# A fused attention and sign-weight FFN layer: partition folds of the dot products, sums of o in rows, signs kept in DRAM, relu values split in another place

## The chip, the cores and the metric

The kernel runs on one core of one Trainium2 chip, as one launch. The metric is the device time in microseconds (us) of that core. Engines are named as in the profile: PE is TensorE's matmul row and PEld its weight loads, DVE is VectorE, ACT is ScalarE, POOL is GpSimd, SP is SyncE. SP and POOL issue the DMAs, and only POOL issues those that add to their destination.

## The reference

x has 2048 tokens of 512 values. All arithmetic is float32.

```python
xn = layernorm(x)
# attention: 16 heads of 128, four lags
q, k, v = (causal_conv4(silu(xn @ W)) for W in (Wq, Wk, Wv))   # depthwise, 4 taps
z, a, b = xn @ Wz, xn @ Wa, xn @ Wb
q, k = rotate(q), rotate(k)                                    # rotary embedding
q, k = q / max(norm(q), 1e-12), k / max(norm(k), 1e-12)        # per head
out = 0
for s in range(4):                                             # k, v, a of s tokens earlier
    attn = sum_d(q * lag(k, s)) / sqrt(128)
    out += attn * sigmoid(lag(a, s) * b) * lag(v, s)
out = out * rsqrt(mean(out * out) + 1e-6) * norm_w * silu(z)   # mean over all 2048 columns
s = out @ Wout
# FFN with weights reduced to their signs
h = relu((xn @ sign(up).T) * up_scale)
g = silu((h @ sign(down).T) * down_scale * output_scale)
return x + s * g
```

## The kernel before, in words

**Layout.** Channels lie on partitions and tokens in columns. The 2048 tokens are four blocks of 512 (TB), the 16 heads eight pairs (NP). A pair's 256 channels are two halves j of 128 partitions; partitions 0 to 63 of both halves are the first head, 64 to 127 the second. xnT holds the normalised tokens, transposed.

**Order of work.** Tile decides the order on ACT, POOL and SP; `InOrder` (L68) keeps PE and DVE in the order in which the program is written, and gives all their instructions line 76, so that groups are told apart by tile names. The stages are:

- *Front stage.* `step(p, -1)` (L524) for p = 0 to 7 makes queries and keys of block 0: `queries` (L297) projects q, convolves it; `products` (L320) does the same for k, turns q for the lags (L305), squares q and k, and multiplies q by the lagged k. Beside it the FFN of block 0 is computed in four groups of G = 4 chunks: in even steps `ups` (L617), the first two chunks between q and k (`beside_q`), the last two after the step; in odd steps `downs` (L623), likewise in halves. `fetch` (L605) loads raw weights, ACT makes their signs (L612). `in_two_terms` (L576) splits a relu value into hid_hi and hid_lo on DVE (a cast and a subtraction), both of which PE multiplies.
- *Main loop.* `step(p, b)` for b = 0 to 2 makes q and k of block b+1 and the rest of block b: `values` (L434), z (L441), `weighted` (L450: the four lags of v times coefficients broadcast from DRAM, tiles bc, te, o), oz = o times norm_w times silu(z) (L481), and every second step the output projection of two pairs (L495), whose results (part, three buffers) POOL adds up in s_dram (L513, L515).
- *Last attention block.* L667 to L734: values, z and outputs of block 3. Beside it the up weights are loaded once more and reduced to signs (up_raw, L686 to L693), two chunks per step, and two chunks of the next FFN block are computed ahead (L728).
- *FFN of blocks 1 to 3.* L737 on: down weights are loaded and reduced to signs (L741), then for each chunk f up (ph), relu, split, down (pf). `ends` (L744) does the final gating.

**Dot products.** `products` multiplies q by four lags of k into pr (128 partitions, 4 lags x 512 tokens), once for each half j (L342 to L347). In blocks 1 to 3 POOL's DMA adds the second to the first (L349); in block 0, made in the front stage, DVE does (L352). `sum_dots` (L371) then sums over partitions on PE, pair by pair and a step later: four matmuls with a 32-column indicator `of_head`, one for each lag, in the four column tiles, all pairs accumulating in one bank. `coefficients` (L423) multiplies the dots by the norms and the gate and writes them to DRAM.

**Sums of o.** The squares of o are added over pairs by POOL's DMA (L478). `sums_of_o` (L379) sums them over partitions at the end of a block: eight matmuls with the squares as weights and one column of ones, giving tokens on partitions in so, copied to ss_acc. After the last block ACT and DVE turn ss_acc into rms (L733, L734), in DVE's order ahead of the FFN's splits.

**Queues.** POOL issues its DMAs in order, an instruction that waits holds those behind it; so does SP. In the main loop POOL's are sq<-sq, pr<-pr, ss<-o, s_dram<-part, and at some steps ab_dram and xnT.

Of the kernel before, what the change touches and what calls it, by code (L numbers as in the profile page):

```python
# [44 lines left out]
P = 128  # L45
# [36 lines left out]
def recurrent_layer(ctx: ExitStack, tc: tile.TileContext, a: dict, out: bass.AP):  # L82
# [11 lines left out]
    ones = const.tile([P, 1], F32, name="ones")  # L94
# [12 lines left out]
    ab_dram = dram.tile([LW, HALO + S], F32, name="ab_dram")  # L107
    f_dram = dram.tile([TB, HID], F32, name="f_dram")
# [19 lines left out]
    def small_loads():  # L128
        nc.sync.dma_start(conv_w, a["conv_w"])
        nc.sync.dma_start(w_ab, a["w_ab"])  # L130
        nc.sync.dma_start(ab_dram[:, 0:HALO], no_ab)
        nc.sync.dma_start(turns, a["turns"])
        nc.sync.dma_start(of_head, a["of_head"])
        nc.sync.dma_start(norm_w, a["norm_w"])
        nc.sync.dma_start(up_scale, a["up_scale"])
# [37 lines left out]
    def statistics(b, c):  # L173

        if c == 0:
            means[b] = qks.tile([P, TC, 2], F32, tag="mv", name=f"mv{b}", bufs=2)
            nc.sync.dma_start(xnT[:, :, HALO + b * TB : HALO + (b + 1) * TB], a["xT"][b])
        t = b * TC + c
        x_in = qks.tile([P, HID], F32, tag="x_in", name=f"x_in{t}", bufs=2)
        nc.sync.dma_start(x_in, a["x"][t * P : (t + 1) * P, :])  # L180
        st = qks.tile([P, 6], F32, tag="st", name=f"st{t}", bufs=2)
        dve.bn_stats(st, x_in)
        dve.bn_aggr(means[b][:, c, :], st)
# [43 lines left out]
    def gate(b):  # L227

        g = qks.tile([P, TB], F32, tag="gate", name=f"gate{b}", bufs=2)
        other = qks.tile([P, TB], F32, tag="rk", name=f"gate_b{b}", bufs=1)  # L230
        for r in range(0, P, H):
            lo = HALO + b * TB - r // LW
            nc.sync.dma_start(g[r : r + H, :], ab_dram[0:H, lo : lo + TB])
            nc.sync.dma_start(other[r : r + H, :], ab_dram[H:, HALO + b * TB : HALO + (b + 1) * TB])
        dve.tensor_tensor(g, g, other, ALU.mult)
        nc.scalar.activation(g, g, AF.Sigmoid)
        gates[b] = g
# [82 lines left out]
    def products(p, b, q, between=None):  # L320

        n = f"_{p}_{b}"
        load(qks, "k", p, b)
        q0 = q[:, LAGS - 1]
        k = with_halo(qks, "k", "k", 1, p, b)
        raw = raw_of(qks, "k", p, b)
        if p % 2 == 0:
            sum_squares()
        convolve(1, p, raw, k[:, :, HALO:])
        keep_halo("k", k, p, b)  # L330
        if between:
            between()
        turn(q)

        sq = [qks.tile([P, 2, TB], F32, tag=f"sq{j}", name=f"sq{j}" + n, bufs=2 - j) for j in range(2)]
        for j in range(2):
            nc.scalar.activation(sq[j][:, 0], q0[:, j], AF.Square)
            nc.scalar.activation(sq[j][:, 1], k[:, j, HALO:], AF.Square)
        nc.gpsimd.dma_start(sq[0], sq[1], accum_op=ALU.add)
        squares_due.append((p, sq[0]))  # L340
        prs = []
        for j in range(2):  # L342
            pr = qks.tile([P, LAGS, TB], F32, tag="pr", name=f"pr{j}" + n, bufs=2)
            k0 = k[:, j, 0:TB]
            k_lags = bass.AP(k0.tensor, k0.offset, [k0.ap[0], [1, LAGS], k0.ap[1]])
            dve.tensor_tensor(pr, q[:, :, j, :], k_lags, ALU.mult)
            prs.append(pr)  # L347
        if b:
            nc.gpsimd.dma_start(prs[0], prs[1], accum_op=ALU.add)  # L349
        else:  # L350

            dve.tensor_tensor(prs[0], prs[0], prs[1], ALU.add)  # L352
        dots_due.append((p, prs[0]))

    def add(to, s, p, src, start, stop):

        rows = to[LW * s : LW * s + LW, :]
        pe.matmul(rows, of_head[:, p, :], src, start=start, stop=stop, tile_position=(0, LW * s))

    def sum_squares():  # L360

        if not squares_due:
            return
        if squares_due[0][0] == 0:
            banks["squares"] = sums.tile([P, TB], F32, tag="squares", name="squares")
        for p, sq in squares_due:
            for i in (1, 0):
                add(banks["squares"], 2 * (p % 2) + 1 - i, p, sq[:, i, :], p < 2, p >= NP - 2)
        squares_due.clear()

    def sum_dots():  # L371

        p, pr = dots_due.pop(0)
        if p == 0:
            banks["dots"] = sums.tile([P, TB], F32, tag="dots", name="dots")
        for s in range(LAGS):
            add(banks["dots"], s, p, pr[:, LAGS - 1 - s, :], p == 0, p == NP - 1)

    def sums_of_o(b):  # L379

        so = mm.tile([P, TC], F32, tag="mm", name=f"so{b}")
        for c in range(TC):
            for j in range(2):
                pe.matmul(
                    so[:, c : c + 1],
                    squares[b][:, j, c * P : (c + 1) * P],
                    ones,
                    start=(j == 0),
                    stop=(j == 1),
                )  # L390
        nc.scalar.copy(ss_acc[:, b * TC : (b + 1) * TC], so)  # L391
# [4 lines left out]
    def norms(b):  # L396

        sqs = banks["squares"]
        r = qks.tile([P, HALO + TB], F32, tag="r", name=f"r{b}", bufs=1)[0 : 2 * LW]
        nc.scalar.copy(r[0:LW, 0:HALO], kept_r)  # L400
        sq2 = qks.tile([2 * LW, TB], F32, tag="sq2", name=f"sq2{b}", bufs=1)
        nc.scalar.copy(sq2, sqs[2 * LW :, :])
        norm = r[:, HALO:]
        dve.tensor_tensor(norm, sq2, sqs[0 : 2 * LW, :], ALU.add)
        dve.tensor_scalar_max(norm, norm, NORM_MIN * NORM_MIN)
        nc.scalar.activation(norm, norm, AF.Sqrt)
        rows[b] = r
# [33 lines left out]
    def gates_of_output(p, b):  # L441

        load(vs, "z", p, b)
        wo = vs.tile([P, 2, HID], F32, tag="wo", name=f"wo_{p}_{b}", bufs=3)
        nc.sync.dma_start(wo, a["wo"][p])
        z = vs.tile([P, 2, TB], F32, tag="z", name=f"z_{p}_{b}", bufs=1)
# [77 lines left out]
    def step(p, b, beside_q=None):  # L524
# [9 lines left out]
        due = len(dots_due)  # L534
        products(p, b + 1, q, (lambda: norms_in_rows(b)) if change and b else None)
        if change:
# [4 lines left out]
            due = 0  # L541
# [5 lines left out]
        if due:  # L547
            sum_dots()
# [53 lines left out]
    with tc.tile_pool(name="pre", bufs=1, side="right") as pre:  # L602
        signs = {}

        def fetch(g, which):  # L605

            for f in range(G * g, G * g + G):
# [4 lines left out]
                nc.scalar.activation(sign, raw, AF.Sign)  # L612
                signs[which, f] = sign
# [30 lines left out]
        for p in range(NP):  # L644
            g = p // 2
            if p == 0:
                step(p, -1)
                fetch(0, "up")
                ups(0, G)
            elif p % 2 == 0:  # L650
                step(p, -1, lambda: ups(G * g, G * g + 2))
                ups(G * g + 2, G * g + G)
            else:
                step(p, -1, lambda: downs(g, 0, 2))
                downs(g, 2, TC)
# [24 lines left out]
    up = ffw.tile([P, NFC, KC, P], F32R, name="up")  # L680
    first_down = ffw.tile([P, 2, HID], F32R, name="first_down")
# [4 lines left out]
    def fetch(to, name, src, shape):  # L686

        raw = ffw.tile(shape, F32, tag="raw", name=name, bufs=4)
        nc.sync.dma_start(raw, src)
        return lambda: nc.scalar.activation(to, raw, AF.Sign)  # L690

    def fetch_up(f):
        return fetch(up[:, f], f"up_raw{f}", a["up"][f], [P, KC, P])  # L693

    def fetch_down(to, f):
        return fetch(to, f"down_raw{f}", a["down"][f], [P, HID])

    def ups_ahead(f, ph):
        hids.append((1, f, up_projection(ph, ffw, f, 1, up[:, f], xs)))


    fetched = []
    for p in range(NP + 1):
        if 0 < p < NP:
            load(vs, "v", p, last)
            raw = raw_of(vs, "v", p, last, 1)
        if p:
            z, wo = gates_of_output(p - 1, last)
        if p % 2 == 1:
            output_projections()  # L710
        if p < NP:
# [5 lines left out]
        for sign in fetched:  # L717
            sign()
        if p < NP:
            fetched = [fetch_up(2 * p), fetch_up(2 * p + 1)]  # L720
        else:
            fetched = [fetch_down(first_down[:, f], f) for f in range(2)]
        if p == 4:
            xs = in_two_terms(ffw, tokens(1), "xs", 1, [P, KC, TB], "xs1")
    for sign in fetched:
        sign()
# [10 lines left out]
    with tc.tile_pool(name="ff", bufs=1, side="right") as ff, tc.tile_pool(  # L737
        name="ph", bufs=3, space=PSUM
    ) as phs, tc.tile_pool(name="pf", bufs=1, space=PSUM) as pfs:
        down = ff.tile([P, NFC - 2, HID], F32R, name="down")  # L740
        for f in range(2, NFC):  # L741
            fetch_down(down[:, f - 2], f)()
# [32 lines left out]
        def down_projection(c, f, terms):  # L775
            for i, term in enumerate(terms):
# [3 lines left out]
                    first_down[:, f] if f < 2 else down[:, f - 2],  # L780
# [5 lines left out]
        for b in range(1, NTB):  # L786
            pf = [pfs.tile([P, HID], F32, name=f"pf{c}") for c in range(TC)]
            for f in range(2, NFC + 2):
# [3 lines left out]
                if ub < NTB:  # L792
                    ph = phs.tile([P, TB], F32, name="ph")
                    hids.append((ub, uf, up_projection(ph, ffw, uf, ub, up[:, uf], xs)))
                if b == 1 and f == 2:
                    scale, gate = ends(0)
                if b == 1 and f in (4, 6, 8, 10):
                    scale(f // 2 - 2)
                    gate(f // 2 - 2)
# [12 lines left out]
            if b == last:  # L812

                for cs in (0, 1), (2, 3):
# [41 lines left out]
def _constants():  # L856
# [9 lines left out]
    of_head = (row[None, None, :] == 2 * np.arange(NP)[None, :, None] + half[:, None, None])  # L866
    return {
        "turns": turns.astype(f),
# [23 lines left out]
```

## Time and profile before

| what | value |
|---|---|
| median of 3 runs | 1468.28 us (1465.31 to 1468.89) |
| the profiled execution, device time | 1469.35 us |
| its span in the profile | 1467.6 us |
| granted TensorE clock, mean | 0.99 |
| front stage, first ph to first pv | 27.8 to 237.4 us |
| main loop, to the last block's first pv | 237.4 to 1084.5 us |
| last attention block, to its last po | 1084.5 to 1280.1 us |
| FFN of blocks 1 to 3, to the last pf | 1282.2 to 1459 us |
| two software and hardware DMA queues | 81.80 MB and 161.84 MB |

How to read it: times in the trace are counted from the span's start. A row of a group reads line, engine, operation, out<-in, shapes and count, then busy us, mean ns of one, and the idle time just before. One float32 matmul of 512 columns gives two records, one of the sign-weight FFN (fp32r) one. "A <- B" among the waits means that A's engine stood still until B was done. The DMA share is the mean busy share of the 16 DMA engines.

### The profile page before, as it was taken

To read this page: it belongs to the slowest core of one execution; us is meant where nothing else is said; L and a number is where in the kernel's file an instruction comes from. 1 tells how busy PE (TensorE), PEld (TensorE's weight loads), DVE (VectorE), ACT (ScalarE), POOL (GpSimd) and SP (SyncE) were. 2 spreads that over 40 slices of the span, in tenths; PEclk is the share of its full clock that TensorE was granted. 3 is DMA by queue.
4 is the path that set the end of the run, shared out by engine and by line. 5 is a ranking of instruction groups with operands and counts; after the bars stand their busy time and mean duration, and the time that the engine had idled before them with its cause. 6 is when DMAs were issued, how large, how long until landed. Compare 5 with 4: busy or idle time off the path is not lost. (4 is left out here: it accounts for less than half of the span.)

```text
span 1467.6 us, 12650 instructions
## 1 busy us (share of the span) xinstructions
PE 1428.4 (97%) x4080; PEld 699.4 (48%) x4080; DVE 1184.2 (81%) x1327; ACT 631.5 (43%) x1213; POOL 160.0 (11%) x205
## 2 busy tenths in 40 slices
PE   7999889999999999999999999999998999999997
PEld 4545444434444444444444444444434444578886
DVE  6888889999999878999898689998886968245454
ACT  6456445444444444444444444434343433242122
POOL 0101101010201110102011101010100011100000
PEclk9999999999999999999999999999999999999999
DMA  8747538877888677768886787687748976562120
GB/s 277 203 101 152 121 74 214 198 203 189 189 218 176 153 172 192 194 169 188 212 185 147 159 208 192 169 181 184 162 101 200 256 239 151 84 224 68 40 87 29
DMA packets 95857, 244.44 MB, mean 167 GB/s; under 512 B 15344, under 2 KB 15728, under 8 KB 92720
## 3 DMA queue, kind: packets, MB, share of 16 engines
q1 hardware_dynamic: 71024, 161.84, 36.1%
q0 software_dynamic: 24768, 81.80, 30.7%
q8 instruction: 32, 0.52, 0.1%
q14 instruction: 33, 0.27, 0.1%
HBM read 157.60 MB, written 27.28 MB: 126 GB/s over the span
## 5 line engine op out<-in xcount | busy, mean ns | idle before, releaser
L76 PE MATMUL pz<-xnT,wz 128*128 128x512 f32 x512 | 228.2, 598 | 4.5 <-ACT up L690 4.5
L76 PE MATMUL po<-wo,oz 128*128 128x512 f32 x512 | 225.6, 598 | 3.2 <-DVE oz L76 3.2
L76 PE MATMUL pq<-xnT,wq 128*128 128x512 f32 x512 | 228.0, 598 | 0.7 <-ACT xnT L169 0.7
L76 PE MATMUL pv<-xnT,wv 128*128 128x512 f32 x512 | 226.7, 595 | 0.9 <-ACT up L690 0.9
L76 PE MATMUL pk<-xnT,wk 128*128 128x512 f32 x512 | 225.3, 592 | 0.0
L76 DVE SCALAR_TENSOR_TENSOR q<-rq,conv_w,q 128x512 f32<-128x512 f32 x192 | 141.9, 749 | 49.9 <-ACT q L280 45.3
L76 DVE SCALAR_TENSOR_TENSOR k<-rk,conv_w,k 128x512 f32<-128x512 f32 x192 | 143.0, 751 | 45.8 <-ACT k L280 41.2
L76 PEld LDWEIGHTS po<-wo,oz 128*128 128x128 f32 x512 | 96.9, 191 | 130.6 <-issue 112.8
L76 PEld LDWEIGHTS pz<-xnT,wz 128*128 128x128 f32 x512 | 96.1, 190 | 132.3 <-issue 117.3
L76 DVE SCALAR_TENSOR_TENSOR v<-rv,conv_w,v 128x512 f32<-128x512 f32 x192 | 141.4, 750 | 20.8 <-ACT v L280 16.2
L76 PEld LDWEIGHTS pv<-xnT,wv 128*128 128x128 f32 x512 | 95.4, 189 | 129.7 <-issue 114.8
L76 PEld LDWEIGHTS pq<-xnT,wq 128*128 128x128 f32 x512 | 97.7, 191 | 122.9 <-issue 119.4
L76 PEld LDWEIGHTS pk<-xnT,wk 128*128 128x128 f32 x512 | 96.7, 189 | 121.1 <-issue 116.6
L76 DVE TENSOR_TENSOR pr<-q,k 128x2048 f32<-128x2048 f32 x64 | 143.8, 2288 | 1.1
L76 DVE SCALAR_TENSOR_TENSOR q<-q,turns 128x1024 f32<-128x1024 f32 (+1 forms) x128 | 127.1, 1014 | 2.3
L76 DVE TENSOR_TENSOR o<-o,te 128x1024 f32<-128x1024 f32 x96 | 117.6, 1225 | 3.3
L76 DVE TENSOR_TENSOR te<-v,bc 128x1024 f32<-128x1024 f32 x96 | 117.0, 1219 | 0.0
L597 ACT ACTIVATE hid<-ph,up_scale 128x512 f32<-128x512 f32 x64 | 43.9, 685 | 116.2 <-PE ph L76 115.7
L76 DVE CAST hid_hi<-hid 128x512 fp32r<-128x512 f32 x64 | 27.1, 424 | 76.3 <-ACT hid L597 76.3
L268 ACT ACTIVATE rq<-pq 128x512 f32<-128x512 f32 x64 | 38.1, 596 | 111.3 <-PE pq L76 111.1
L509 ACT COPY part<-po 128x512 f32<-128x512 f32 x64 | 37.2, 582 | 97.5 <-PE po L76 68.8
L76 PE MATMUL ph<-xs_hi,up 128*128 128x512 f32 x192 | 76.7, 399 | 0.3 <-ACT ss_acc L391 0.3
(128 smaller groups left out, 1612.9 us busy)
## 6 DMA issues: line engine op xcount, KB each, us to landing
bc<-co_dram SPq DMA_DIRECT2D x128, 256.0 KB, 5.5
pr<-pr POOLq DMA_DIRECT2D x24, 1024.0 KB, 8.3
wq<-in_wq_dram SPq DMA_DIRECT2D x32, 512.0 KB, 4.3
wk<-in_wk_dram SPq DMA_DIRECT2D x32, 512.0 KB, 4.7
sq<-sq POOLq DMA_DIRECT2D x32, 512.0 KB, 5.3
wv<-in_wv_dram SPq DMA_DIRECT2D x32, 512.0 KB, 6.5
wz<-in_wz_dram SPq DMA_DIRECT2D x32, 512.0 KB, 4.7
wo<-in_wo_dram SPq DMA_DIRECT2D x32, 512.0 KB, 8.4
```

The source lines that it names most:

```text
L76: return self.tc.keep_in_program_order(getattr(self.engine, op)(*args, **kwargs))
L268: nc.scalar.activation(to[:, j, :], pp, AF.Silu)
L509: nc.scalar.copy(part, po)
L597: nc.scalar.activation(hid, ph, AF.Relu, scale=up_scale[:, f : f + 1])
```

## The change

- A pair's products are folded over partitions by POOL's DMAs before PE sums them: within each head's 64 partitions, the second 32 are added to the first 32. An even pair stays in its own tile. An odd pair is copied into the second 32 of the even pair's tile and its own second 32 added there, so that one group of four matmuls (indicator `of_heads`) sums both pairs. There are 16 groups instead of 32.
- In blocks 1 to 3 only even pairs have their halves j added by DMA. Odd pairs, and all pairs of block 0, do it on DVE: the second product is made two lags at a time into a half-sized tile and added at once.
- In the front stage the second half of `ups` or `downs` moves into `products` (`beside_k`), between the turning of q and the squares and products.
- `sums_of_o` takes the squares as the moving operand: two matmuls with 32 columns of ones, one for each half, in two column tiles. ACT copies the rows, POOL writes one to DRAM and adds the other, SP loads the sum back with tokens on partitions.
- The front stage stores the signs in DRAM. Later loads read them (1 MB each, four for up, one for the first four down chunks, three for the rest) instead of raw weights, and there is no sign activation there.
- In the last attention block weights of v, z and the output are asked for earlier. In the FFN, the gating of block 0 stands two chunks later, and the last two column blocks of the end are finished one at a time.
- To make room, x_in and gate have one buffer, and sq2 uses rk's.

```diff
+    of_heads = const.tile([P, NP // 2, LW], F32, name="of_heads")
+    ones = const.tile([P, LW], F32, name="ones")
...
         turn(q)
+        if beside_k:
+            beside_k()
...
+        pr = qks.tile([P, LAGS, TB], F32, tag="pr", name="pr0" + n, bufs=2)
+        product(pr, 0, 0, LAGS)
+        if b and p % 2 == 0:
+            pr1 = qks.tile([P, LAGS, TB], F32, tag="pr", name="pr1" + n, bufs=2)
+            product(pr1, 1, 0, LAGS)
+            nc.gpsimd.dma_start(pr, pr1, accum_op=ALU.add)
         else:
+            for lo in range(0, LAGS, 2):
+                half = qks.tile([P, 2, TB], F32, tag="half", name=f"half{lo}" + n, bufs=1)
+                product(half, 1, lo, lo + 2)
+                dve.tensor_tensor(pr[:, lo : lo + 2], pr[:, lo : lo + 2], half, ALU.add)
+        for h in range(0, P, D // 2):
+            first, second = slice(h, h + D // 4), slice(h + D // 4, h + D // 2)
+            if p % 2 == 0:
+                nc.gpsimd.dma_start(pr[first], pr[second], accum_op=ALU.add)
+            else:
+                both = dots_due[-1][1]
+                nc.gpsimd.dma_start(both[second], pr[first])
+                nc.gpsimd.dma_start(both[second], pr[second], accum_op=ALU.add)
...
     def sum_dots():
+        if not dots_due or not dots_due[0][2]:
+            return
...
+        so = mm.tile([P, TB], F32, tag="mm", name=f"so{b}")
+        for j in range(2):
+            add(so, j, ones, squares[b][:, j], True, True)
+        row = vs.tile([P, HID], F32, tag="part", name=f"so_sb{b}", bufs=3)
+        nc.scalar.copy(row[0 : 2 * LW], so[0 : 2 * LW])
+        nc.gpsimd.dma_start(ss_dram[b : b + 1], row[0:1])
+        nc.gpsimd.dma_start(ss_dram[b : b + 1], row[LW : LW + 1], accum_op=ALU.add)
+        nc.sync.dma_start(
+            ss_acc[:, b * TC : (b + 1) * TC], ss_dram[b].rearrange("(c p) -> p c", p=P)
+        )
...
                 nc.scalar.activation(sign, raw, AF.Sign)
+                nc.gpsimd.dma_start(signs_dram[which][:, f], sign)
...
             elif p % 2 == 0:
-                step(p, -1, lambda: ups(G * g, G * g + 2))
-                ups(G * g + 2, G * g + G)
+                step(p, -1, lambda: ups(G * g, G * g + 2), lambda: ups(G * g + 2, G * g + G))
...
+        if p < NFC // G:
+            some = slice(G * p, G * p + G)
+            nc.gpsimd.dma_start(up[:, some], signs_dram["up"][:, some])
+        elif p == NFC // G:
+            nc.gpsimd.dma_start(first_down, signs_dram["down"][:, 0:NFD])
...
-                for cs in (0, 1), (2, 3):
+                for cs in (0, 1), (2,), (3,):
```

## The prediction

> **What bounds the kernel now.** I read the page first, then TensorE's waits, then the windows by stage, then the timeline around each wait. The page's own lines:
>
> ```profile
> PE 1428.4 (97%) x4080; PEld 699.4 (48%) x4080; DVE 1184.2 (81%) x1327; ACT 631.5 (43%) x1213; POOL 160.0 (11%) x205
> ...
> PE   7999889999999999999999999999998999999997
> PEld 4545444434444444444444444444434444578886
> DVE  6888889999999878999898689998886968245454
> ```
>
> TensorE is busy 97% of 1467.6 us, so its work is the bound, but VectorE is in the nines through the middle and is the next bound. TensorE's idle time is 39 us, and the waits say for whom (total us, times, longest):
>
> ```profile
> PE pf L76 <- DVE hid_hi L76: 13.5, 4, 5.2
> PE tp L76 <- DVE x_in L76: 6.8, 3, 6.0
> PE pz L76 <- ACT up L690: 4.5, 1, 4.5
> ```
>
> The first is the front stage (steps of block -1), the third the last attention block. The windows give busy us of PE, PEld, DVE, ACT and POOL, then clock, DMA share and GB/s; the front stage, then the main loop in thirds:
>
> ```profile
> 27.60:231.20 203.60, 189.03 (x601) 100.84 (x600) 173.87 (x189) 106.99 (x213) 28.67 (x35) 0.96 0.57 138
> 231.20:515.00 283.80, 281.94 (x728) 117.98 (x727) 263.95 (x284) 135.41 (x274) 36.35 (x44) 0.99 0.80 196
> 515.00:790.00 275.00, 275.00 (x717) 116.83 (x716) 245.49 (x264) 125.65 (x256) 36.28 (x44) 1.00 0.76 184
> 790.00:1065.00 275.00, 275.00 (x712) 117.22 (x711) 242.58 (x258) 119.73 (x227) 32.80 (x40) 1.00 0.75 177
> ```
>
> VectorE's idle time is 29.7 us in the front stage, then 19.8, 29.5 and 32.4. The rows the sum uses (busy, mean ns):
>
> ```profile
> L76 DVE TENSOR_TENSOR pr<-q,k 128x2048 f32<-128x2048 f32 x64 | 143.8, 2288 | 1.1
> ...
> L76 DVE TENSOR_TENSOR te<-v,bc 128x1024 f32<-128x1024 f32 x96 | 117.0, 1219 | 0.0
> ```
>
> ```profile
> L76 PE MATMUL dots<-pr,of_head 128*32 128x512 f32 x256 | 34.0, 603 | 0.0
> ...
> L76 PE MATMUL so<-ones,ss 128*128 128x1 f32 x64 | 7.4, 245 | 0.0
> ```
>
> **Dot sums and products.** A group of dots is followed 0.99 us later by the next matmul (301.78 to 302.77 in the timeline). 32 groups become 16: 15.8 us of TensorE, 4 groups in the front and 12 in the main loop. VectorE pays. An odd pair of blocks 1 to 3 replaces its second 2048-wide product (2.29) by four 1024-wide operations (te row, 1.22): +2.59 us, 12 times, 31.1 us in all, 10.4 per block. In block 0 a product and an addition (4.58) become 4.88: +0.3, 8 times, 2.4 us.
>
> **Relu values split sooner (front stage).** Today the last two hid values of an even step are split after both products and their addition, so the next pf waits. From the start of pq to that of pk in the four odd steps, the timeline has 15.46, 16.43, 18.94 and 17.08 us where pq and half the pf matmuls need 6.87 + 3.73 = 10.60: 25.5 us lost (waiting, and records 0.43 instead of 0.23 us apart after it). With the splits ahead of the products, VectorE reaches them some 7 us earlier. TensorE would then need per two steps 27.5 (pq, pk) + 14.9 (ph, pf) + 0.9 + 1.0 = 44.3 us, VectorE 2 x (4.5 + 4.5 + 4.05 + 7.2 + 0.87) + 4.4 = 46.6. So VectorE takes over as the bound: I count on its idle time, 29.7, of which some 10 stay (start, ln, k<-ACT), and 2.4 is added: **-17 us**. Bounds: -29.5 if both TensorE terms (25.5 and 4 x 0.99) show; 0 if the same wait only moves.
>
> **Main loop.** TensorE loses 12 dots groups and most of three so groups (below), 14.4 us. VectorE gains 10.4 per block. In the first third that takes 19.8 idle to 9.4, and the backlog from the front comes on top: I give no gain. In the other two, idle falls to 19 and 22, still more than the first third has now at full TensorE pace: -3 and -4. **-7 us**; bounds -14.4 (VectorE always follows) and +31.1 (none of its additions fits a gap).
>
> **Folds on POOL.** An odd pair now sends two copies and, after they land, two accumulations; the dots of an even step wait for them. Behind them in POOL's queue stand sq, ss and the s_dram parts; part has three buffers, so ScalarE, then PSUM, would be next. Today an odd pair's products are done (its pr issue) at 359.04 and 649.77, and the even step's dots run at 377.86 and 669.88: 18.8 and 20.1 us, of which 2.6 go to the longer products. One round is 0.9 us of issue twice plus a landing between 4.1 (f_dram<-f, 256 KB) and 7.4 us (xnT<-ln_dram, accumulated in SBUF, 256 KB); copies beside accumulations: I take 5, so 2 x (0.9 + 5) = 12. It fits by 4 us: cost 0; at 7.4 twice it is 16.6 and just fails to be hidden. The Trainium skill's "DMA: Bandwidth & Descriptors", section "Anatomy of one DMA", gives 2.0 us plus the bytes over 436 GB/s, an estimate of 2.6 us for such a transfer; two rounds would be 7 us by it, issue included, and the folds would never be seen. The rows here are slower than it in every case.
>
> **Sums of o.** A so group takes 1.77 us (538.41 to 540.11); four matmuls of squares in column tiles take 0.9 to 1.0, two such at most that: 4 x 0.85 = 3.4 saved, three of them counted above. But the sums now pass through DRAM, and before the FFN VectorE's reciprocal of rms stands ahead of the splits of hid 2. From the end of the last po: so 0.95, ScalarE's copy 0.58, a write and an accumulation 3.0 each (two ab_dram accumulations start at 229.52 and 232.53), the load of 512 4-byte pieces, then sqrt, reciprocal and cast 0.3 + 0.25 + 0.43. Nearest rows for the load: up_scale 2.8 us, and the writes in the same pieces:
>
> ```profile
> ln_dram<-ln SPq DMA_DIRECT2D x6, 2.0 KB, 9.9
> ```
>
> That makes 11.3 to 18.4 us, while TensorE has so and three ph and two pf of 1.87, to 10.3. It waits 1.0 to 8.1, plus about 1.5 of slow records, and loses today's 1.84 + 0.25 + 1.4 less 0.95. Net 0 to +7.1; the DMA share there is 0.34 against 0.5 and more beside the ln row, so I take a load of 6.3: **+3.5 us**. The same page's fit would make the load 2.0 us and the net about -0.8; its section "Rules for kernel authors" says, against this edit, that a last dimension that is not contiguous is lowered to one descriptor per element, and gives no price for it.
>
> **Signs in DRAM.** 32 stores in the front (256 KB, POOL, 0.6 to 0.9 us each) lie beside work; 32 sign activations of 0.63 leave ScalarE. In the last block TensorE loses 7.5 us today: pz and pv start at 1136.10 and 1145.84 instead of 1131.44 and 1138.31, their weights having been issued at 1126.07 and 1139.97 behind bc and up_raw loads. The change asks for them a step earlier, but POOL sends 5 MB of signs at once when the DMA share is already 1.02 (1120 to 1130). Bounds -7.5 and +7.5 (one more such wait); nearer the first, since two of three weight buffers are then filled beforehand: **-4 us**.
>
> **Tail and rest.** The last two column blocks are finished one by one: at most one scale operation, **-0.7 us**. x_in and gate with one buffer, sq2 in rk's: each is loaded once a step or block, read long before; 0, and up to +3.7 (what SP waits today for st). One more constant load: 0 to 0.4.
>
> **Sum.** 1467.6 - 17 - 7 + 3.5 - 4 - 0.7 = 1442.4 of span; the execution took 1469.35, so 1.75 on top, 1444. That execution lies 1.1 above the median, 1468.28; I let it stand.
>
> **Rivals.**
> 1. VectorE decides from the front on: it keeps its gaps (k<-ACT, 24.3 us there), and the wait of pf moves instead of going. Front -5, main loop 0, the rest as above: 1467.6 - 5 - 1.2 + 1.75 = 1463. For: 263.95 busy of 283.8 right behind. Against: in the first third VectorE does run with few gaps.
> 2. All TensorE work shows: front -29.5, main -14.4, last block -7.5, seam 0, tail -0.7: 1417. Against: 46.6 against 44.3 per two steps.
> 3. Slower: the folds arrive late at the even step's dots. The point is a chain of 16 us (18.8 less 2.6). At landings of 8.3 us, those of the 1 MB pr accumulation, the chain is 18.4 + about 2 of queueing: 4 to 5 us at each of 12 dots, +54, 1444 + 54 = 1498; with landings of 7.5 about +1 each and still faster. For: DMA share 0.75 to 0.80, folds added to it; the last pair of a block has only 16.2 us (500.47 to 516.71). Against: a quarter of pr's bytes.
> 4. The edits cancel (main loop +10 to +20 from VectorE's 31.1, front -17): within 1464 to 1472.
>
> **Chances.** Forecast (1432 to 1456) 0.50; rival 1 (1456 to 1464) 0.17; rival 2 (below 1432) 0.11; rival 4 0.08; rival 3 and any other slower 0.14. A measurement tells 0.3%, 4.4 us, from no change: faster 0.78, same 0.08, slower 0.14. The range leaves out half of rival 2 and most of rival 3: 1424 to 1474.
>
> **What would show it.** Right: pf's wait for hid_hi under 5 us; the front stage (to the first pv) ends 15 to 20 us earlier, with VectorE idle near 10 there; dots x128 near 17 us; four idle us before the third pf of the FFN, put down to rms; no dots wait on pr. Wrong: dots waiting on DMA pr<-pr in even steps (rival 3); VectorE above 97% in every third with TensorE waiting for oz (rival 1); pv or pz waiting on weights beside the up load.

## The result, and the profile after

The changed kernel takes **1490.1 us** (median of 4 runs, 1487.2 to 1492.1) against 1468.2 before (1465.3 to 1468.9): ratio 1.0151, 95% interval 1.0127 to 1.0176. It is slower by 22 us, where 24 us less was forecast; the range of 1424 to 1474 did not hold it. The profiled execution has a span of 1490.3 us, 22.7 more than before.

The page of the changed kernel, the same lines as before: busy time by engine, and the 40 slices.

```profile
PE 1404.0 (94%) x3904; PEld 686.7 (46%) x3904; DVE 1215.9 (82%) x1379; ACT 610.3 (41%) x1181; POOL 245.8 (16%) x337
...
PE   8958993999998999999999999999979899999997
...
DVE  6878887799999897999999989999992998336454
```

TensorE has 24 us less work and the kernel is longer: idle time grew from 39 to 86 us. Slices 3, 4 and 7 of TensorE's row, all nines before, fall to 5, 8 and 3 (the front stage), and in the last block slices 30 and 32, nines before, fall to 7 and 8, with a 2 in VectorE's slice 31 between them, where a 6 stood. TensorE's waits (total us, times, longest one):

```profile
PE dots L76 <- issue: 23.4, 1, 23.4
PE dots L76 <- DMA pr<-pr: 21.5, 5, 15.8
PE po L76 <- DVE oz L76: 9.8, 3, 7.7
PE pz L76 <- DMA wz<-in_wz_dram: 8.3, 1, 8.3
PE dots L76 <- DVE q L76: 6.7, 1, 6.7
...
PE pf L76 <- DVE hid_hi L76: 0.8, 1, 0.8
```

The wait of pf for hid_hi, 13.5 us before, is gone, as forecast. In its place the dots wait, 51.6 us over the span. TensorE's timeline shows that the four groups of the front stage have 46.7 of them (start, busy, and in brackets the idle time before the group and what was put down as ending it):

```profile
93.07 1.93 PE L76 MATMUL dots<-pr,of_heads 128*32 128x512 f32 x8 [15.81 <-DMA pr<-pr]
...
145.78 1.93 PE L76 MATMUL dots<-pr,of_heads 128*32 128x512 f32 x8 [6.72 <-DVE q L76]
...
193.49 1.07 PE L76 MATMUL dots<-pr,of_heads 128*32 128x512 f32 x8 [0.76 <-DMA pr<-pr]
...
255.12 1.93 PE L76 MATMUL dots<-pr,of_heads 128*32 128x512 f32 x8 [23.40 <-issue]
```

All four wait for folds: "q" and "issue" are only what the profile named. GpSimd's last addition of each group landed 0.1 to 0.3 us before the dots began (for the second group it was issued at 138.72 and landed 6.8 us later, for the fourth at 247.70 and 7.2 us later). Records are also slower just after the longer waits: the group takes 1.93 instead of 1.07 us.

Four landmarks of TensorE cut the span into stages. "Front" is to the first pv, "main" to the first pv of the last block, "last" to the end of that block's last po, "rest" what is left of the span. The stages are those of the profiled execution, the times are medians. The experiments told of below are in the same table: names with a_ are edits of the changed kernel, those with b_ of the kernel before, and best_1, best_1_main_folds and best_2 are put together from parts of both. The ratios are to the kernel before as timed beside each of them (medians of 1468.0 to 1470.1 us).

| kernel | front | main | last | rest | time, us | ratio to before, 95% |
|---|---|---|---|---|---|---|
| before | 237.4 | 847.2 | 195.8 | 187.3 | 1468.2 | |
| after | 257.0 | 839.7 | 207.4 | 186.2 | 1490.1 | 1.0127 to 1.0176 |
| b_relu_only | 211.1 | 849.5 | 198.2 | 187.1 | 1446.4 | 0.9808 to 0.9876 |
| b_folds_only | 255.5 | 843.3 | 205.0 | 189.8 | 1491.2 | 1.0104 to 1.0203 |
| b_rows_only | 235.9 | 846.3 | 199.2 | 192.2 | 1474.4 | 1.0017 to 1.0038 |
| b_early_only | 237.3 | 847.8 | 188.2 | 186.6 | 1461.6 | 0.9927 to 0.9951 |
| a_front_per_pair | 215.6 | 849.4 | 207.1 | 186.2 | 1460.0 | 0.9916 to 0.9964 |
| a_no_sign_store | 250.3 | 836.4 | 195.0 | 187.1 | 1472.2 | 1.0007 to 1.0040 |
| a_dots_later | 246.4 | 836.4 | 211.5 | 186.5 | 1478.3 | 1.0039 to 1.0081 |
| a_spread | 258.2 | 838.1 | 195.4 | 186.3 | 1479.5 | 1.0043 to 1.0085 |
| a_no_folds | 212.2 | 846.3 | 201.9 | 186.4 | 1447.8 | 0.9837 to 0.9870 |
| best_1 | 211.9 | 846.4 | 189.8 | 186.8 | 1437.7 | 0.9770 to 0.9799 |
| a_ab_later | 257.4 | 836.4 | 209.5 | 186.4 | 1490.9 | 1.0120 to 1.0173 |
| a_relaxed | 234.2 | 839.2 | 197.6 | 188.4 | 1461.1 | 0.9920 to 0.9951 |
| a_ab_later_2 | 251.1 | 840.6 | 208.0 | 186.4 | 1487.5 | 1.0102 to 1.0156 |
| a_relaxed_2 | 231.6 | 837.2 | 195.7 | 188.4 | 1456.8 | 0.9898 to 0.9948 |
| best_1_main_folds | 215.5 | 848.7 | 199.9 | 187.2 | 1453.5 | 0.9878 to 0.9937 |
| best_2 | 211.7 | 847.8 | 188.2 | 186.7 | 1436.6 | 0.9763 to 0.9806 |

So the loss is +19.6 us in the front and +11.6 in the last block, against -7.5 in the main loop and -1.1 in the rest. The forecast had -17, -4, -7 and, for seam and tail together, +2.8.

**Theory**: in the front stage the folds come too late for the dots, each group for its own reason, and undo what the relu split gains. **Rivals**: the relu split itself makes VectorE the bound there; or the sign stores on GpSimd's queue hold up all folds.

### The profile page after: what moved, and what is told of

Its sections match the earlier page's. It is cut to its first block, busy times and chain, and to the rows that moved or that the text cites. A ratio compares the mean times of both kernels' runs of the same rounds, so it can differ in the third digit from the quotient of the medians.

```text
span 1490.3 us, 12569 instructions
## 1 busy us (share of the span) xinstructions
PE 1404.0 (94%) x3904; PEld 686.7 (46%) x3904; DVE 1215.9 (82%) x1379; ACT 610.3 (41%) x1181; POOL 245.8 (16%) x337
## 4 chain that ended last, share of the span: by engine, by line
PE 46%; DVE 33%; DMA 8%; issue 8%; ACT 3%; POOL 1%; SPq 1%; DVEq 0%; POOLq 0%; ACTq 0%
PE po L76 9%; DVE q L76 9%; PE pz L76 7%; PE ph L76 6%; PE pf L76 6%; PE pv L76 6%; PE pq L76 6%; DVE k L76 5%; PE pk L76 5%; DMA pr<-pr 4%; DVE pr L76 4%; DVE o L76 3%; DVE te L76 3%; DVE v L76 3%; DVE half L76 2%
## 5 line engine op out<-in xcount | busy, mean ns | idle before, releaser
L76 PE MATMUL po<-wo,oz 128*128 128x512 f32 x512 | 228.9, 605 | 9.8 <-DVE oz L76 9.8
L76 DVE TENSOR_TENSOR pr<-q,k 128x2048 f32<-128x2048 f32 x44 | 99.7, 2289 | 9.7 <-DMA pr<-pr 8.5
L76 PE MATMUL ph<-xs_lo,up 128*128 128x512 f32 x192 | 75.8, 395 | 0.0
```

Of the source, the lines that this page charges most:

```text
L76: return self.tc.keep_in_program_order(getattr(self.engine, op)(*args, **kwargs))
```

## Experiments in the front stage

**Block 0 without folds** (a_front_per_pair).

```diff
+        if not b:
+            dots_due.append([p, pr, "alone"])
+            return
         for h in range(0, P, D // 2):
...
-            add(banks["dots"], s, of_heads[:, p // 2], src, p == 0, p == NP - 2)
+            heads = of_head[:, p] if alone else of_heads[:, p // 2]
+            add(banks["dots"], s, heads, src, p == 0, p == NP - (1 if alone else 2))
...
```

> The changed kernel, but block 0 (the front stage) sums the dots pair by pair with of_head, without folds; blocks 1 to 3 keep folds and pairing. Theory (late folds in the front stage cost the time): the waits of the dots on folds there, 46.7 us in four groups, go, four more groups of dots of about 8.5 us each come back, and the first pv starts 20 to 37 us earlier than the 257.0 us of the changed kernel, at 220 to 237; the rest stays, so 1453 to 1470 us. Rival (the relu values split sooner make VectorE the bound of the front stage whatever the folds do): first pv at 245 to 257, time 1478 to 1490.

Measured: 1460.0 us, first pv at 215.6; no dots wait is left in the front. The 41.4 us that it starts earlier are, but for about 1 us, the 46.7 of waits less four more groups of about 1 us (the 8.5 us for each in the expectation was wrong, so the front ends earlier than expected; eight records take 1.07). That settles the place. What was not expected: the main loop gives 9.7 us back.

**The relu split alone** (b_relu_only): the kernel before, with beside_k as in the change's diff and nothing else.

> The kernel before with one part of the change: the second half of the ups and downs moved between turn and the squares. Theory (the split itself was priced rightly at -17 in the front stage and the folds took it away): first pv at 216 to 224 instead of 237.4, TensorE's wait for hid_hi before pf under 8 us, 1448 to 1455 us. Rival (VectorE becomes the bound and nothing is won): first pv at 234 to 240, 1465 to 1471 us.

Measured: 1446.4 us, 22.6 less; first pv at 211.1, and this is all that is left of pf's wait for hid_hi:

```profile
PE pf L76 <- DVE hid_hi L76: 0.6, 1, 0.6
```

The rival that has VectorE as the new bound falls: TensorE is busy in the whole of the front stage and VectorE is idle for 8 us of it (window, length, busy us of PE, PEld, DVE, ACT and POOL, then clock, DMA share and GB/s):

```profile
27.60:211.10 183.50, 183.50 (x622) 97.06 (x620) 175.54 (x194) 110.13 (x218) 28.34 (x35) 1.00 0.67 164
```

The forecast's -17 was even too small (-26.3 in the front stage, of which the later stages give back 4.5).

**Folds alone** (b_folds_only): the kernel before with products, folds, pairing and the buffers that they need.

> The kernel before with folds, pairing and the buffers they need, and nothing else of the change (relu split as before, signs by ScalarE, o's squares in columns). Theory: in the front stage the dots wait for the folds with GpSimd's queue free of sign stores too, 20 to 45 us of waits on folds, in part in place of the waits for hid_hi; first pv at 240 to 262; the main loop 5 to 10 us shorter; 1465 to 1485 us. Rival (folds are hidden, the loss comes from the other parts): no wait on folds over 5 us, first pv at 230 to 238, 1455 to 1463 us.

Measured: 1491.2 us, more than either theory had. The front's four waits are 6.66, 7.25, 4.72 and 15.00 us, 33.6 together, with no sign store in the queue. The front ends at 255.5, within 1.5 us of the changed kernel's: **where there are folds, they set the pace, and little is left of what the relu split gains**. Folds and relu split together, without the sign stores, end the front at 250.3 (a_no_sign_store, next): beside folds the split gains 5.2 us there instead of 26.3, and the sign stores take 6.7 back. The same folds cost 22 us alone and 42 on top of the other edits (1490.1 against a_no_folds, 1447.8).

**Without sign stores** (a_no_sign_store): raw loads and ScalarE's signs in the last block and the FFN again, two down chunks ahead instead of four.

```diff
                 nc.scalar.activation(sign, raw, AF.Sign)
-                nc.gpsimd.dma_start(signs_dram[which][:, f], sign)
...
```

> The changed kernel without the signs in DRAM: the last block and the feed-forward stage load raw up and down weights again and ScalarE takes the sign there; the weights of the output gates are still loaded early. Theory (each of the front stage's late dots has its own cause, and the sign stores on GpSimd's queue stand only in the first): the first wait of 15.8 us falls to 5 to 10, the last of 23.4 stays, first pv at 245 to 254; the last block loses its 8.3 us wait for wz; 1472 to 1488 us. Rival (the sign stores are what holds up all folds): all four waits nearly gone, first pv at 215 to 225, 1450 us or less.

Measured: 1472.2 us. The waits become 8.15, 2.75, 2.13 and 23.65: the stores lengthen the first two (the theory had only the first), and the rival (they hold all folds) falls. Two views of the changed kernel show the first wait. GpSimd's timeline; the odd pair's products were done at 68.5, and its copies are the third line:

```profile
63.27 0.54 POOL L641 DMA_DIRECT2D down_signs<-pre_down  x1 [2.98 <-ACT kept_rq L259]
78.48 0.53 POOL L641 DMA_DIRECT2D up_signs<-pre_up  x1 [14.67 <-ACT pre_up L640]
79.00 1.00 POOL L372 DMA_DIRECT2D pr<-pr  x2
85.21 0.81 POOL L373 DMA_DIRECT2D pr<-pr  x1 [5.21 <-DMA pr<-pr]
86.73 0.78 POOL L373 DMA_DIRECT2D pr<-pr  x1 [0.71 <-DMA pr<-pr]
```

ScalarE's timeline, the sign that the store waited for:

```profile
77.55 0.63 ACT L640 ACTIVATE pre_up<-pre_up_raw 128x512 fp32r<-128x512 f32 x1 [13.10 <-DMA pre_up_raw<-in_up_dram]
```

A queue that keeps its order lets a store of something not yet made stand ahead of folds whose products were ready 10.5 us earlier.

**Dots of the front one projection later** (a_dots_later).

```diff
         if p % 2 == 0:
             sum_squares()
+        elif not b and p > 1:
+            sum_dots()
...
-        if p and p % 2 == 0:
+        if b >= 0 and p and p % 2 == 0:
             sum_dots()
```

> The changed kernel, but in the front stage the dots of a pair group stand one projection pair and one block of ups or downs later (behind the odd step's pk instead of behind the even step's ups); folds, their queue and the last group (behind step 7) are as in the change. Theory (only the distance from fold to dots is too short in the front stage): the first three waits, 23 us together, go and the last of 23.4 us stays; first pv at 228 to 240 instead of 257.0; since the main loop was seen to give back some 10 us when the front stage ends 41 us earlier, 1468 to 1480 us. Rival (the folds hold the front stage through VectorE's buffers or work, not through the dots): waits move to other tiles, first pv at 247 to 260, 1483 to 1492 us.

Measured: 1478.3 us, first pv at 246.4, between the two. The first three waits go and the last is 16.6; but 12.5 us of waiting for hid_hi come back, as the rival said. Of VectorE's waits there, the longest is 8.0 us on ScalarE's q (ScalarE stood 10.3 us for pre_up_raw), and two, 6.8 us together, are on pr's buffers. Distance helps. That the transfers which folds and stores add are the next brake fits these waits, and without the stores (a_relaxed, below) the wait for hid_hi is 4.3 us; the part of the folds in it is not shown.

**The last group.** In the changed kernel, GpSimd's timeline before the fourth wait; pair 7's products were done at 233.6:

```profile
223.95 0.85 POOL L227 DMA_DIRECT2D ab_dram<-ab_sb  x1
230.36 0.76 POOL L229 DMA_DIRECT2D ab_dram<-ab_sb  x1 [5.55 <-DMA ab_dram<-ab_sb]
236.93 0.76 POOL L229 DMA_DIRECT2D ab_dram<-ab_sb  x1 [5.81 <-DMA ab_dram<-ab_sb]
242.64 0.76 POOL L229 DMA_DIRECT2D ab_dram<-ab_sb  x1 [4.95 <-DMA ab_dram<-ab_sb]
243.17 1.26 POOL L372 DMA_DIRECT2D pr<-pr  x2
246.52 0.80 POOL L373 DMA_DIRECT2D pr<-pr  x1 [2.09 <-DMA pr<-pr]
247.70 0.78 POOL L373 DMA_DIRECT2D pr<-pr  x1 [0.39 <-DMA pr<-pr]
```

The folds stand behind the gate's chained additions of block 1. Two runs put them ahead:

```diff
-        ab = qks.tile([P, TB], F32, tag="rk", name=f"ab_sb{b}", bufs=1)
+        ab = qks.tile([P, TB], F32, tag="x_in" if b == 1 else "rk", name=f"ab_sb{b}", bufs=1)
+        queue = pool if b == 1 else nc.gpsimd
...
+                queue = pool if b == 0 and p == NP - 1 else nc.gpsimd
+                queue.dma_start(both[second], pr[first])
+                queue.dma_start(both[second], pr[second], accum_op=ALU.add)
```

> The changed kernel, but at the end of the front stage the folds of pair 7 stand ahead of the four gate transfers of block 1 (ab_dram) on GpSimd's queue instead of behind them; the gate transfers use another buffer so that nobody waits for theirs. Theory (the last group of dots of the front stage waits because its folds stood 10 us behind that chain): the copies go out at about 234 instead of 243.2, the wait of 23.4 us falls to 11 to 15, first pv at 246 to 250, 1479 to 1487 us. Rival (the two rounds of folds themselves, or a queue of transfers, are the wait): wait 20 or more, first pv at 254 or later, 1487 to 1492 us.

Inconclusive: the kept order ran copy, addition, copy, addition, so the second half's copy (one of two issues from 243.82 on) stood behind the landing of the first half's, and the wait stayed at 21.4 us, 1490.9 us. The same with both copies first (a_ab_later_2):

> The changed kernel with the folds of pair 7 ahead of the gate transfers of block 1, both copies first and then both additions (in the run before this one the second copy stood behind the first addition, so that the two halves of the fold ran one after the other). Theory (the last wait of the front stage is 10 us of standing behind the gate transfers and some 12 us of two chained folds): copies at about 234 to 237, wait 11 to 15 instead of 23.4, first pv at 246 to 250, 1479 to 1486 us. Rival (the chain of two folds alone): wait 20 or more, 1488 to 1493 us.

Measured: copies at 232.73, 10.4 us earlier, but dots at 249.26, only 5.9 earlier; wait 18.7, between the two; 1487.5 us, an interval that overlaps the change's. The chain itself grew from 12.0 us (243.17 to 255.12) to 16.5. The 23.4 us of the changed kernel are thus 1.9 in which pair 7's products did not even exist (TensorE reaches the dots at 231.7), 9.6 of queue and 12.0 of folds; but taking the queue away gave back only 5.9, a quarter, since the folds then took longer. Why they did is not shown.

**All three eased** (a_relaxed, with the wrong order of a_ab_later in it, and a_relaxed_2): no sign stores, dots later, folds ahead of the gate.

> The changed kernel without signs in DRAM, with the front stage's dots later and with the folds of pair 7 ahead of the gate transfers: all three causes of the late dots eased at once, folds in all blocks. Theory (folds can be had without loss only where a step lies between fold and dots, and behind pair 7 there is none): only the last group still waits, 8 to 15 us, first pv at 222 to 234, main loop 838 to 848, last block 194 to 197; 1446 to 1460 us, over the 1437.7 of the version without folds. Rival (once they have room folds pay): first pv at 218 or less, main loop 840 or less, 1436 us or less.

> The changed kernel without signs in DRAM, with the front stage's dots later, and the folds of pair 7 ahead of the gate transfers in the order copies, then additions. Theory: the last group's wait falls from the 15.7 us of the version with the wrong order to 7 to 11, first pv at 224 to 230, 1452 to 1458 us: still 15 us or more over the version without folds. Rival (with all room given folds cost nothing): 1442 us or less.

Measured: 1461.1 and 1456.8 us, first pv at 234.2 and 231.6, last waits 15.7 and 13.3, the only dots waits left in the front. The first lies just outside its theory, the second is inside it in time, with a longer wait than the 7 to 11 us expected; neither rival holds. Eased as far as these edits go, folds still cost 19 us against the kernel without them (best_1, 1437.7).

## Experiments behind the front stage

**No folds at all** (a_no_folds) **and no signs in DRAM either** (best_1). The first is the change with the products, dots and steps of before; the second takes the sign stores out as well.

> The changed kernel without folds and pairing (dots pair by pair in all blocks, product halves added as before); relu split, rows of o, signs in DRAM and early weights as in the change. Theory (folds cost the front stage 40 us and buy next to nothing in the main loop, since with an equally early start it took 849.4 us with them and 849.6 without): first pv at 211 to 217, main loop 847 to 851, last block 197 to 203 with the burst still in it, rest 186; 1441 to 1454 us. Rival (folds do shorten the main loop by their 12 groups of dots, and the other parts cost the front stage): main loop 858 or more or first pv over 230, 1460 us or more.

> The changed kernel without folds and without signs in DRAM: relu values split sooner, o's squares in rows, weights of the output gates early, the last downs in three parts. Theory: front stage 211, main loop 849.5, last block 186 to 193 (the early weights bought 8 to 11 us where no burst stood against them), rest 186 to 188; 1433 to 1441 us, below both kernels. Rival (the early weights only pay while folds make the last block start late): last block 197 to 200, 1443 to 1449 us, no better than the relu split alone.

Measured: 1447.8 and 1437.7 us, both as the theory had it. best_1 beats both kernels, 0.9785 of before. Its largest waits of TensorE, to set against those of the change:

```profile
PE tp L76 <- DVE x_in L76: 6.9, 3, 6.3
PE po L76 <- DVE oz L76: 3.7, 2, 2.3
PE pf L76 <- ACT down L706: 1.5, 1, 1.5
```

Signs in DRAM cost 10 us here, and 18 in the changed kernel (a_no_sign_store), of which 6.7 in the front.

**Folds in blocks 1 to 3 alone** (best_1_main_folds): best_1 with the edit of a_front_per_pair in place of no folds.

> The version without folds and signs in DRAM, with folds and pairing in blocks 1 to 3 alone. Theory (in the main loop the folds take 12 groups of dots, 12.5 us, from TensorE and give VectorE about 2.7 us in each of 12 odd steps, 32 us, so nothing is won; and the last block's first po waits 7.7 us for oz): first pv at 211 to 216, main loop 846 to 850, last block 193 to 197; 1442 to 1449 us, against 1437.7. Rival (folds pay in the main loop as the prediction had it, 7 us): 1428 to 1434 us.

Measured: 1453.5 us, 15.8 more than best_1 and more than expected. The windows of the main loop (length, then busy us of PE, PEld, DVE, ACT and POOL); first best_1:

```profile
211.90:1058.30 846.40, 844.08 (x2156) 354.55 (x2153) 765.16 (x817) 384.69 (x761) 110.16 (x133) 1.00 0.76 181
```

and with folds:

```profile
215.50:1064.20 848.70, 834.00 (x2061) 354.69 (x2058) 789.70 (x847) 382.24 (x761) 147.79 (x189) 0.99 0.82 188
```

Folds take 10.1 us from TensorE and give VectorE 24.5; TensorE's idle time goes from 2.3 to 14.7, and the loop is 2.3 us longer. Of TensorE's waits in that window 7.6 us are po for oz, VectorE's work, and 7.1 are dots, each of which began 0.1 to 0.3 us after the last fold had landed: folds come late in the main loop too. VectorE also ends the loop later: the last block's po waits 7.7 us for oz, as in every run here that has folds, instead of 1.4, and that block is 10.1 us longer. The front is 3.5 longer too. The shorter main loop of the changed kernel is thus no gain that an early front stage would keep: there VectorE has 778.5 us of work left inside the loop's window instead of 789.7, and has done 204.5 us before the first pv, where it did 192.5.

**The burst in the last block** (a_spread).

```diff
-        if p < NFC // G:
-            some = slice(G * p, G * p + G)
-            nc.gpsimd.dma_start(up[:, some], signs_dram["up"][:, some])
+        if p < NP:
+            some = slice(2 * p, 2 * p + 2)
+            pool.dma_start(up[:, some], signs_dram["up"][:, some])
...
-            nc.gpsimd.dma_start(squares[b], o2, accum_op=ALU.add)
+            pool.dma_start(squares[b], o2, accum_op=ALU.add)
```

> The changed kernel with the 4 MB of up signs in the last block asked for 0.5 MB at a time, each behind the squares of one pair on GpSimd's queue, instead of four 1 MB transfers in one burst (and the first down signs at the end instead of in that burst). Theory (the burst delays the weights of z and the bc rows): TensorE's 8.3 us wait for wz goes, the last block is 6 to 11 us shorter, 1478 to 1485 us. Rival (the place of the loads is indifferent; folds or the order of the weights cost it): last block within 2 us of the 207 of the change, 1487 to 1492 us.

Measured: 1479.5 us; the wait for wz is gone and the last block takes 195.4 instead of 207.4. In the changed kernel GpSimd sent 5 MB in 3 us:

```profile
1136.47 2.24 POOL L744 DMA_DIRECT2D up<-up_signs  x4
1138.68 0.56 POOL L746 DMA_DIRECT2D first_down<-down_signs  x1
```

and 18 us later VectorE still waited for bc rows that SP had asked for at 1135.78 and 1138.07. Rows of bc issued between 1136 and 1142 us landed after 18.5 us (median of six; 6.0 over the whole run), and the weights of z after 19.9. SP meanwhile stood 12.8 us at further bc loads with the next weights behind them:

```profile
1156.26 1.23 DVE L76 TENSOR_TENSOR o<-v,bc 128x1024 f32<-128x1024 f32 x1 [18.95 <-DMA bc<-co_dram]
```

With the spread loads the same line's wait is 6.99 us. The wait of 18.95 us is the 2 in VectorE's slice 31.

**The early weights alone** (b_early_only): the kernel before, with v, z and wo of the last block asked for a step earlier.

> The kernel before with the weights of v, z and wo of the last block asked for one step earlier, and nothing else. Theory (this is where the version without folds and without signs in DRAM gains its 9 us on the relu split alone): pv and pz no longer wait behind ScalarE or for wz in the last block, last block 186 to 191 instead of 195.8; 1459 to 1464 us. Rival (it pays only together with the rows of o or the parts at the end): 1466 to 1470 us.

Measured: 1461.6 us, last block 188.2: 7.6 us shorter.

**o's squares in rows alone** (b_rows_only), and the best version without them (best_2: relu split, early weights, last downs in three parts).

> The kernel before with o's squares summed in rows, and nothing else. As priced in the prediction: 3.5 us slower (0 to 7.1), 1468 to 1475 us, with TensorE's wait for rms at the seam. Rival (the seam is covered by the first ups and downs of the feed-forward stage): TensorE's wait before the first pf that rms decides stays under 2 us, and 1465 to 1469 us.

> The kernel before with the relu split sooner, the early weights of the last block and the last downs in three parts; o's squares in columns as before. Theory (the rows cost the 4 us that they cost alone): 1432 to 1436 us. Rival (beside the early weights the rows are free): 1436 to 1440 us, as with them.

Measured: alone the rows cost 4.3 us (2.5 to 5.6), partly in another place than priced: in the last block pz waits 7.7 us for wz, and at the seam pf waits 1.6 and 1.8 us. best_2 takes 1436.6 us, and its ratio to before is that of best_1, 0.9785: beside early weights the rows cost nothing that can be told, and my theory there fell.

## Why the prediction was wrong, step by step

- **"It fits by 4 us: cost 0" (folds on POOL) is the step that failed.** The slack of 18.8 and 20.1 us was read at two places of the main loop and used for all 16 groups. There it held nearly: the main loop's waits on folds are 4.9 us in all, and 10.6 and 7.1 where the front stage is early (a_front_per_pair, best_1_main_folds). The front stage has no v, z and po between an odd pair's products and the dots of the next step, and the trace of before showed it. VectorE's timeline of before, pair 3's last addition (ends at 125.03):

```profile
122.74 2.29 DVE L76 TENSOR_TENSOR pr<-pr,pr 128x2048 f32<-128x2048 f32 x1
```

TensorE's timeline of before, the dots that would now need it folded:

```profile
133.42 1.04 PE L76 MATMUL dots<-pr,of_head 128*32 128x512 f32 x8
```

  That is 8.4 us; pairs 1 and 5 have 8.0 each, pair 7 has 5.3. My own chain of 12 us fits none of them: 4.0 + 3.6 + 4.0 + 6.7 = 18 us of waiting stood in that trace, before any queueing. Measured alone: 33.6. The price of the folds was about right: from the first copy to the dots they took 14.1, 15.6, 11.2 and 12.0 us in the changed kernel's four groups. The room was wrong.
- **The relu split, -17**: the wait for hid_hi goes, as forecast, but the limit put behind it was wrong. VectorE does not take over: alone, TensorE is busy in all of the front's 183.5 us and VectorE in 175.5, and the gain is 22.6 us (26.3 in the front stage, above the 25.5 that the forecast had as this term's bound). In the change nothing of it is left, because the next thing to be late was the folds, not VectorE.
- **Rival 3** had the mechanism (folds late at even steps' dots) at the wrong 12 groups, with the price put on landing times. The four groups it left out decided.
- **POOL's queue** was checked for what stands behind the folds, not for what stands ahead of them. Two things did: a sign store (10.5 us in the first group) and the gate's chain (9.6 in the last).
- **Main loop, -7**: -7.5 measured, and right by accident. With the front stage early, as forecast, folds make it 2.3 us longer, nearest to rival 1: of 14.7 us of TensorE's idle time, 7.6 are for VectorE's oz (its added work: 31.1 forecast, 24.5 seen in the window) and 7.1 for folds.
- **Last block, -4**: +11.6. The two effects weighed there were real: early weights alone save 7.6 us in that block, the burst costs 12.0 (207.4 against 195.4). I took a value near the first, although the same paragraph named 5 MB at a DMA share of 1.02. The wait for oz, 7.7 us, was not in the sum.
- **Sums of o, +3.5**: 2.5 to 5.6 alone, so right alone in size. In the change 1.7 us of waiting is left at the seam. The load of ss_acc in 4-byte pieces took 2.2 us (median), not the 6.3 that I took from the ln row. The fit in the Trainium skill's "DMA: Bandwidth & Descriptors", section "Anatomy of one DMA", is for transfers that GpSimd issues; the forecast's 2.0 by it is near this load, but SyncE issues it. For the folds, which GpSimd issues, the fit gave an estimate of 2.6 us where the median landing was 6.0.
- **Readings**: a so group takes 1.70 us by the two times given for it, not 1.77; f_dram's median landing is 3.9, not 4.1; and the DMA share at the seam before is 0.74 (1280 to 1300 us), not 0.34. The first is worth 0.3 us in the sum, the second nothing; the third was the reason for taking a load of 6.3.

## What to carry to other kernels

A slack is a property of one place: before a transfer is put between a producer and its consumer, measure the distance at every stage where the pair occurs, in the trace before the change, and begin with the shortest step. When a stall is taken out, ask what is late next by working out the distance of the new dependences in that same stage; here one edit gained 22.6 us alone, and another cost 42 us beside it. On a queue that keeps its order, look at what stands ahead of the new entry and what that waits for, and send bulk loads in pieces tied to the work.

## What the runs showed of the hardware

- How long the folds take differs from place to place: two chained rounds of two 256 KB transfers took 11.2 to 15.6 us from the first copy to the dots in the changed kernel's four groups, and 16.5 in the last group when they were sent 10 us earlier (a_ab_later_2; 12.0 before).
- Issuing was slower where the DMA engines were busier: SP took 0.42 us to issue each small load of the gate (32 KB) at a DMA share of 0.30 (b_folds_only, 56 to 62 us), and 1.05 to 2.25 us in the changed kernel at a share of 1.01 (56 to 66 us). The raw weights behind them were asked for at 73.65 there and at 66.63 in a_front_per_pair: 7.0 of the 13.1 us for which ScalarE waited for them.
- After a wait TensorE is slow for a while: dots took 1.93 us after waits of 6.7 us and more and 1.07 after 0.76, and the front stage's granted clock was 0.92 in the changed kernel against 1.00 in b_relu_only.
